# Letting ScalarE or VectorE copy Strassen banks out of PSUM, and three more stages of the last pairs turned on TensorE

## The chip, the core and the metric

The kernel runs on one core of a Trainium2 chip. The core has five engines, each with its own in-order queue: TensorE (PE, with its weight loads PEld), VectorE (DVE), ScalarE (ACT), GpSimd (POOL), and SyncE (SP), which here only issues DMAs. The metric is the device time of one execution in microseconds (us); lower is better.

## What is computed

There are 128 graphs of 128 nodes with 512 features. Four graph-attention layers follow each other, and each is added to its input and normalised over the features. In every layer the attention scores are a sum of two vectors, passed through a leaky ReLU, masked by the adjacency matrix and put through a softmax:

```python
x = _layernorm(x + L0(x, adj))   # attention on x itself, one head
x = _layernorm(x + L1(adj, x))   # two GAT layers inside: x@W1 (512->1024, 4 heads), elu, h@W2 (1024->512)
x = _layernorm(x + L2(x, adj))   # x@W (512->8 heads of 64), 8 heads of attention
x = _layernorm(x + L3(x, adj))   # scores from x@W_fc, attention on x, elu
# each attention:
e = leaky_relu(s_src[:, :, None] + s_dst[:, None, :], 0.2)
attn = softmax(where(mask, e, -inf)); out = attn @ h
```

All arithmetic is float32.

## The kernel before

The 128 graphs are handled as 64 pairs. A pair passes four stages, written as `first`, `second`, `third` and `fourth` in the kernel, with a dense projection between each two: by w1 after `first`, by w2 after `second`, by w3 after `third`. For a projection the two graphs of a pair are stacked, so that Strassen's scheme with seven products in place of eight can be used (`strassen`, Winograd's form). The w1 projection is two such schemes (two halves of the columns), w2 and w3 are one each, so a pair runs four schemes, 28 products.

Inside a scheme three PSUM banks are used, `pa`, `pb` and `pc`. I call the products p0 to p6 by the number of the weight slot that they read. p0 is written to `pa`, copied out (`taken`, first copy), and then `pa` is written again by p4, copied out, and added to by p5 and p6; `pb` gets p3, is copied out, and p2 is added; `pc` gets p1. That makes four copies of a scheme (three by `taken`, a last one straight to the result) and three additions (`added`, line 834). Every copy is made by `copied`, whose ScalarE instruction is line 797; the additions are VectorE's. The matmuls of the products are line 789. A product into `pa` or `pb` that follows a copy cannot start before that copy has read the bank. PSUM has 8 banks, and all matmul results of the kernel share them.

The attention of each head is: scores by ScalarE's PReLU into PSUM (line 719), mask and row minimum on VectorE (line 732, or 727 in the plain form), exponential with row sum on ScalarE (line 741), reciprocal (749). The layer's matmuls are lines 858, 949 and 1011, the normalisation is lines 760 to 780.

Two helpers move data across partitions. `spread` lays a column along every partition's row, `turned` transposes a block. Each has two forms. The usual one uses VectorE's 32x32 transposes (lines 638 and 692) and two DMAs by way of DRAM (642 and 648; 696 and 700 or 705). The quick one (`quick[0]` true) uses TensorE: lines 624 and 679, with copies out of PSUM at line 686. Which stages are quick is given by `QUICK`: its first number counts pairs at the start whose `first` is quick, the other four count pairs at the end whose `first`, `second`, `third` and `fourth` are.

The order of all work is computed when the program is built. Every step is an `Op` with an engine, a cost, and the buffers it reads and writes. `plan` gives each a due time from the longest path of costs behind it, stretched by `STRETCH` and shifted by `PACE` for each pair, `FIRST` for the first pairs and `SETUP` for the loading of the weights. `lay_out` then runs the engines forward in a model: of the ops that an engine could start, it takes the one that starts soonest, by due time where several could, not further ahead than `AHEAD`. The resulting order is fixed; on the chip each engine works through its own queue in that order and waits on semaphores. From about the twelfth pair on the order repeats itself exactly from pair to pair, with several pairs in flight at different stages; I call one such repetition a period.

Of the kernel before, what the change touches and what calls it, by code (L numbers as in the profile page):

```python
# [14 lines left out]
ALU = mybir.AluOpType  # L15
AX = mybir.AxisListType

P = 128
# [5 lines left out]

STRETCH, PACE, AHEAD = 1.28, 44.46, 61.8
HOP = {"PE": 0.0, "DVE": 0.0, "ACT": 0.5, "POOL": 1.0, "SP": 2.0}
SEED, SPREAD = 1, 0.0
SETUP = (-32.7, -34.3, 3.7)  # L30
QUICK = (2, 0, 0, 1, 2)
FIRST, LAST = (-64.8, -62.4, -109.6, -113.6, -123.5), ()
BANKS, PRODUCTS = 8, 2
SEES = {"PE": 0.06, "DVE": 0.06, "ACT": 0.06, "POOL": 0.06, "SP": 0.0}
TAIL = {"PE": 0.165, "DVE": 0.09, "ACT": 0.1, "POOL": 0.05, "SP": 0.0}
FLIGHT, LANDS, DESCRIBE = 1.3, 2.0, 0.00083
LANES = 8
SLACK = 2.0
REACH = 0.0
LOADS = (50.0, 12.8)  # L40


class Buf:
# [21 lines left out]
class Op:  # L65
# [3 lines left out]
    def __init__(self, engine, parts, emit, ins, outs, joins=(), uses=(), port=False, dma=0.0, due=0.0, gate=0.0, desc=0):  # L69
        self.desc = desc  # L70
        self.engine, self.emit = engine, emit
        self.parts = parts if isinstance(parts, list) else [parts]
        self.ins, self.outs, self.joins, self.uses = list(ins), list(outs), list(joins), list(uses)
        self.port, self.dma, self.due, self.gate = port, dma, due, gate
        self.lag, self.far = 0.0, 1.0 if any(b.tag.startswith("row") for b in self.ins) else 0.0
# [43 lines left out]
def lay_out(ops):  # L119

    n = len(ops)
    before = needs(ops)
# [11 lines left out]
    ready, ends, starts = [0.0] * n, [None] * n, [0.0] * n  # L134
    issued = [False] * n
    lane, landed, pool_until, vector_until, described = 0.0, [], 0.0, 0.0, 0.0

    def enter(i):
        op = ops[i]
        t = op.gate  # L140
        for q in before[i]:
            o = ops[q]
            if o.engine == op.engine != "SP":
                continue
            e = ends[q]
            t = max(t, (e[0] if len(e) == len(op.parts) > 1 else e[-1]) + SEES[o.engine] + (0.2 if op.engine == "PE" else 0.0))
        ready[i] = t
        insort(waiting[op.engine], (op.due, i))

    for i in range(n):  # L150
        if not missing[i]:
# [3 lines left out]
    while len(out) < n:  # L155
        for e, line in waiting.items():
            if e in choice or not line:
                continue
            free, best, limit = clock[e], None, ops[line_up[low]].due + AHEAD
            if e == "SP" and len(landed) >= LANES:  # L160
                free = max(free, landed[-LANES])
            for due, i in line:
                t = max(free, ready[i])
                if due > limit:
                    break
                if not ops[i].ins and due > limit - AHEAD + LOADS[due > 60.0]:
# [18 lines left out]
        waiting[e].remove((op.due, i))  # L185
        changed = False
        issued[i] = True
        while low < n and issued[line_up[low]]:
# [6 lines left out]
                    scarce[b.tag].pop(0)  # L195
                    changed = True
        now = max(now, t)
        starts[i] = u = t
        if e == "POOL":
            u = max(u, vector_until)  # L200
        got = []
# [27 lines left out]
        for q in after[i]:  # L229
            missing[q] -= 1  # L230
            if not missing[q]:
                enter(q)
                choice.pop(ops[q].engine, None)
        if changed:
            choice.clear()

# [25 lines left out]
def tile_gat_stack(  # L262
# [392 lines left out]
    def turned(srcs, n, moving=False, ordered=False):  # L655
# [5 lines left out]
        if quick[0]:  # L661
            for a, (b, src) in enumerate(srcs):
                if ordered:
                    own = Buf("own", [P, m, P])

                    def order(own=own, src=src, copy=(nc.vector.tensor_copy, nc.scalar.copy)[a % 2]):
                        copy(
                            own.ap.rearrange("p k (r b) -> p k r b", b=4),
                            src().rearrange("p k (b r) -> p k r b", b=4),
                        )  # L670

                    op(("DVE", "ACT")[a % 2], 0.06 + 0.137 * m, order, [b], [own])
                    b, src = own, lambda own=own: own.ap
                for lo in range(0, m, 4):
                    px, w = bank(), min(4, m - lo)

                    def flip(src=src, lo=lo, w=w, px=px):
                        for u in range(w):
                            nc.tensor.transpose(px.ap[:, u * P : (u + 1) * P], src()[:, lo + u, :], ident)

                    def taken(lo=a * m + lo, w=w, px=px, moving=moving, e=(lo // 4 + a) % 2):
                        to, got = o.ap[:, lo : lo + w, :], px.ap[:, : w * P].rearrange("p (h i) -> p h i", h=w)
                        if moving:
                            to = o.ap[:, :, lo : lo + w, :].rearrange("p q h c -> p h q c")
                            got = px.ap[:, : w * P].rearrange("p (h q c) -> p h q c", h=w, q=4)
                        (nc.vector.tensor_copy, nc.scalar.copy)[e](to, got)  # L686
# [24 lines left out]
    def attend(rows, src, mask, scaled=False):  # L711
# [38 lines left out]
        if scaled:  # L750
            op("POOL", 0.13 + 0.23 * nh, lambda: nc.gpsimd.tensor_mul(  # L751
                zz.ap, zz.ap, ri.ap.unsqueeze(2).to_broadcast([P, nh, P])
            ), [zz, ri], [zz])
        return zz, ri

    def norm(ys, plus=0.0):
# [22 lines left out]
        for g, (b, y) in enumerate(ys):  # L779
            op("ACT", 0.715, lambda g=g, y=y: nc.scalar.activation(  # L780
                y(), y(), AF.Identity, bias=mr.ap[:, g : g + 1], scale=rd.ap[:, g : g + 1]
            ), [b, rd, mr], joins=[b])
        return rd, md

    def chain(px, w, lhs, rhs, nk, ins, ready, fresh=True):
# [9 lines left out]

    def copied(px, w, to, joins=(), outs=()):
        op("ACT", 0.04 + w / 1200, lambda: nc.scalar.copy(to(), px.ap[:, :w]), [px], outs, joins)  # L797

    def project(lhs, wa, nk, w, n, to, t, ready):
        for c in range(n):  # L800
# [4 lines left out]
    def sums(left, shape):  # L805
# [4 lines left out]

        def summed(o, what, a, b):
            op("POOL", cost, lambda: nc.gpsimd.tensor_tensor(out=own[o][1](), in0=a[1](), in1=b[1](), op=what), [a[0], b[0]], [s[o]])  # L812

        (a11, a12), (a21, a22) = left
        summed(0, ALU.add, a21, a22)
# [5 lines left out]
    def strassen(left, s, w, nk, wide, cols, to, out, ready):  # L821
# [61 lines left out]
    def first(n):  # L883
# [37 lines left out]
        xT = turned([(b, lambda b=b: wide_rows(b.ap)) for b in x1], 8, ordered=True)  # L921
        for g in G:
            op("POOL", 1.24, lambda g=g: nc.gpsimd.tensor_add(x1[g].ap, x1[g].ap, b2t), [x1[g]], [x1[g]], uses=[b2b])
        return dict(xT=xT, xb=x1, m1=m1)

    def second(st, xl):
# [12 lines left out]
        for g in G:  # L939
            for c in range(2):  # L940
                op("POOL", 1.255, lambda g=g, c=c: nc.gpsimd.tensor_add(  # L941
                    xl[g].ap[:, c, : 2 * FH], xl[g].ap[:, c, : 2 * FH], b1t[:, c * 2 * FH : (c + 1) * 2 * FH]
                ), [xl[g]], [xl[g]], uses=[b1b])
            for c in range(2):
                pa, o = bank(), hT[g][c]

# [42 lines left out]
    def fourth(n, st, xl3):  # L989
# [10 lines left out]
        for g in G:  # L1000
# [4 lines left out]
            for q in range(2):  # L1005
# [16 lines left out]
            op("POOL", 1.17, lambda g=g: nc.gpsimd.tensor_add(  # L1022
                x3[g].ap.rearrange("p (h o) -> p h o", h=H2), z3[g].ap[:, :, :FO], x2[g].ap.rearrange("p (h o) -> p h o", h=H2)
            ), [z3[g], x2[g]], [x3[g]])
            op("DVE", 0.14, lambda g=g: nc.vector.tensor_reduce(
                out=sz.ap[:, g, :], in_=z3[g].ap[:, :, FO:].rearrange("p h s -> p s h"), op=ALU.add, axis=AX.X
            ), [z3[g]], joins=[sz])
# [21 lines left out]
            ), [y, pa], joins=[y])  # L1049
        for g in G:  # L1050
            op("POOL", 1.235, lambda g=g: nc.gpsimd.tensor_add(y.ap[:, g, :], y.ap[:, g, :], x3[g].ap), [y, x3[g]], joins=[y])  # L1051
        norm([part(y, g) for g in G])
        op("SP", 0.5, lambda: nc.sync.dma_start(
            out=out[2 * n : 2 * n + 2].rearrange("g p f -> p g f"), in_=y.ap
# [95 lines left out]
```

## Time and profile before

| | |
|---|---|
| runs shown | 3002.24, 3008.66, 3008.86 us, median 3008.66 |
| profiled execution: own time / span of instructions | 3002.53 / 3000.7 us |
| mean granted TensorE clock | 0.986 |
| busy: PE, PEld, DVE, ACT, POOL | 96%, 79%, 86%, 82%, 75% of the span |
| DMA | 594.74 MB, mean 198 GB/s |
| products w1, w2, w3 (line 789) | 803.3, 824.5, 472.6 us on PE |

A row of the groups gives line, engine, operation, what is written from what, its shape and count, then the total busy time, the mean time of one in ns, and the idle time of the engine ahead of them with what ended it. The mean time of one includes the tail of an instruction that overlaps the next; what an instruction really takes from a queue is the distance from its start to the next start, which the timeline gives. A row of the waits gives who waited for whom, the total, the number of times and the longest.

### The profile page before, as it was taken

Reading aid. Unit: us, or ns where it says so; the run is one execution under the profiler, and the core shown is the slowest. Engines: PE = TensorE matmul, PEld = TensorE weight load, DVE = VectorE, ACT = ScalarE, POOL = GpSimd, SP = SyncE. Lnnn points to the kernel's source line nnn. Section 1 sums busy time; section 2 is a strip of 40 time slices with the busy share of each in tenths; the row PEclk is TensorE's granted clock in tenths of the full one; section 3 lists DMA queues with packets and bytes.
Section 4 is the critical chain, followed back from the end, with each engine's and each line's share of the span. In section 5 each row is a group of like instructions: output and inputs, shape, how many; then the busy total and the mean of one; then the engine's idle time right before and its main releaser. Section 6 shows DMA issues by size and latency. Waiting matters only on the chain.

```text
span 3000.7 us, 56720 instructions
## 1 busy us (share of the span) xinstructions
PE 2884.1 (96%) x14200; PEld 2358.1 (79%) x14200; DVE 2592.1 (86%) x9256; ACT 2448.1 (82%) x8237; POOL 2244.7 (75%) x2855
## 2 busy tenths in 40 slices
PE   6999999999999999999999999999999999999986
PEld 4777778888888888888888888888888888888765
DVE  6788888898898899899889889889889988989875
ACT  3567888888888888888888888888888888888877
POOL 3886777877877787777777777777787777777654
PEclk8999999999999999999999999999999999999997
DMA  4469999999999998999989998999999899999863
GB/s 131 98 166 195 194 202 213 211 210 208 219 203 210 217 209 208 217 206 208 218 202 217 210 205 214 210 215 207 212 216 207 210 214 205 211 218 202 196 148 66
DMA packets 1465475, 594.74 MB, mean 198 GB/s; under 512 B 1251476, under 2 KB 1366932, under 8 KB 1465148
## 3 DMA queue, kind: packets, MB, share of 16 engines
q1 hardware_dynamic: 1464072, 589.54, 86.8%
q8 instruction: 115, 1.88, 0.3%
q14 instruction: 212, 1.74, 0.2%
q10 hardware_dynamic: 1076, 1.58, 0.2%
HBM read 367.88 MB, written 223.13 MB: 197 GB/s over the span
## 4 chain that ended last, share of the span: by engine, by line
PE 53%; ACT 21%; DVE 15%; DMA 5%; issue 4%; POOL 1%; SPq 0%; DVEq 0%; ACTq 0%; POOLq 0%
PE ps L789 37%; ACT ps L719 8%; PE ps L858 7%; PE ps L1011 6%; DVE arena L692 4%; ACT arena L741 3%; ACT arena L780 3%; DVE st L760 3%; ACT arena L956 3%; DVE arena L864 2%; ACT arena L797 2%; DVE arena L834 2%; DMA arena<-in_x_dram 2%; DVE arena L732 1%; DMA arena<-scr 1%
## 5 line engine op out<-in xcount | busy, mean ns | idle before, releaser
L789 PE MATMUL ps<-w2s,arena 128*128 128x257 f32 x3584 | 824.5, 381 | 13.4 <-DVE arena L957 9.8
L812 POOL TENSOR_TENSOR arena<-arena 128x256 f32<-128x256 f32 (+1 forms) x768 | 693.7, 915 | 189.8 <-DMA arena<-scr 114.6
L789 PE MATMUL ps<-w1s,arena 128*128 128x258 f32 x3584 | 803.3, 381 | 1.5 <-DVE arena L686 0.8
L789 PEld LDWEIGHTS ps<-w1s,arena 128*128 128x128 f32 x3584 | 680.1, 190 | 151.1 <-issue 39.9
L789 PEld LDWEIGHTS ps<-w2s,arena 128*128 128x128 f32 x3584 | 679.4, 190 | 148.1 <-issue 33.4
L741 ACT ACTIVATE arena<-arena,nm 128x128 f32<-128x128 f32 x1920 | 741.9, 395 | 14.8 <-DVE nm L732 8.7
L732 DVE CUSTOM_DVE_ANT_0 arena<-ps,arena 128x128 f32<-128x128 f32 x1878 | 520.9, 382 | 187.7 <-ACT ps L719 184.7
L719 ACT ACTIVATE ps<-arena 128x128 f32<-128x128 f32 x1504 | 552.6, 371 | 96.9 <-DMA arena<-row 59.8
L692 DVE STREAM_TRANSPOSE arena<-arena 128x512 f32<-128x512 f32 (+1 forms) x813 | 516.7, 637 | 47.3 <-POOL arena L751 31.2
L789 PE MATMUL ps<-w3s,arena 128*128 128x273 f32 x1792 | 472.6, 399 | 34.9 <-ACT arena L797 27.0
L797 ACT COPY arena<-ps 128x258 f32<-128x258 f32 (+2 forms) x1024 | 346.5, 376 | 190.4 <-PE ps L789 182.0
L780 ACT ACTIVATE arena<-arena,mr,rd 128x512 f32<-128x512 f32 x512 | 394.3, 806 | 31.4 <-POOL mr L776 31.4
L789 PEld LDWEIGHTS ps<-w3s,arena 128*128 128x128 f32 x1792 | 328.0, 191 | 107.5 <-issue 35.1
L858 PE MATMUL ps<-arena 128*128 128x512 f32 x768 | 374.3, 611 | 15.3 <-DVE arena L686 3.9
L741 ACT ACTIVATION_READ_ACCUMULATOR arena<-arena,nm 128x1 f32 x1920 | 372.9, 194 | 0.0
L869 POOL TENSOR_SCALAR arena<-arena 128x256 f32<-128x256 int32 x256 | 297.6, 1162 | 91.6 <-DMA arena<-in_adj_dram 51.1
L834 DVE TENSOR_TENSOR arena<-ps,arena 128x258 f32<-128x258 f32 (+2 forms) x768 | 312.9, 413 | 51.3 <-PE ps L789 45.0
L760 DVE BATCH_NORM_STATS2 st<-arena 128x6 f32<-128x512 f32 x512 | 341.5, 679 | 7.9 <-POOL arena L1022 2.1
L941 POOL TENSOR_TENSOR arena<-arena,b1t 128x512 f32<-128x512 f32 x256 | 320.9, 1283 | 0.3
L732 DVE DVE_READ_ACCUMULATOR2_ANT nm<- 128x1 f32 x1878 | 284.6, 152 | 0.0
L1051 POOL TENSOR_TENSOR arena<-arena 128x512 f32<-128x512 f32 x128 | 161.6, 1265 | 137.9 <-DVE arena L1047 130.3
L949 PEld LDWEIGHTS ps<-arena 128*128 128x128 f32 x2048 | 248.0, 192 | 15.2 <-issue 3.4
(96 smaller groups left out, 3622.2 us busy)
## 6 DMA issues: line engine op xcount, KB each, us to landing
scr<-arena SPq DMA_DIRECT2D x313, 512.0 KB
arena<-scr SPq DMA_DIRECT2D x313, 512.0 KB
arena<-row SPq DMA_DIRECT2D x188, 512.0 KB
arena<-in_x_dram SPq DMA_DIRECT2D x64, 512.0 KB
out_dram<-arena SPq DMA_DIRECT2D x64, 512.0 KB
arena<-row SPq DMA_DIRECT2D x187, 128.0 KB
scr<-arena SPq DMA_DIRECT2D x187, 128.0 KB
arena<-scr SPq DMA_DIRECT2D x187, 128.0 KB
```

Source lines behind the costliest of these rows:

```text
L692: op("DVE", 0.075 + 0.134 * m, lambda a=a, src=src: nc.vector.transpose(zb.ap[:, :, a * m : (a + 1) * m, :].rearrange("p b h c -> p h b c" ...
L719: nc.scalar.activation(z.ap[:, h * P : (h + 1) * P], rows[h][1](), AF.Prelu, bias=src[1]()[:, h : h + 1], alpha=SLOPE)
L732: nc.vector.tensor_tensor_reduce(out=zz.ap[:, h, :].rearrange("p (b a) -> p a b", b=4), in0=z.ap[:, h * P : (h + 1) * P].rearrange("p (a b ...
L741: nc.scalar.activation(zz.ap[:, h, :], zz.ap[:, h, :], AF.Exp, bias=nm.ap[:, h : h + 1], scale=-1.0, accum_out=rs.ap[:, h : h + 1],)
L760: op("DVE", 0.585, lambda g=g, y=y: nc.vector.bn_stats(st.ap[:, g, :], y()), [b], joins=[st])
L780: op("ACT", 0.715, lambda g=g, y=y: nc.scalar.activation(y(), y(), AF.Identity, bias=mr.ap[:, g : g + 1], scale=rd.ap[:, g : g + 1]), [b, ...
L789: nc.tensor.matmul(px.ap[:, :w], lhsT=lhs(k), rhs=rhs(k), start=(fresh and k == 0), stop=(k == nk - 1), skip_group_check=True,)
L797: op("ACT", 0.04 + w / 1200, lambda: nc.scalar.copy(to(), px.ap[:, :w]), [px], outs, joins)
L812: op("POOL", cost, lambda: nc.gpsimd.tensor_tensor(out=own[o][1](), in0=a[1](), in1=b[1](), op=what), [a[0], b[0]], [s[o]])
L834: op("DVE", 0.05 + wide / 960, lambda: nc.vector.tensor_add(to(g, h), px.ap[:, :wide], u.ap[:, :wide]), [px, u], joins=[out[g]])
L858: op("PE", 0.885, lambda: nc.tensor.matmul(pa.ap.rearrange("p (s c) -> p s c", s=2) if paired else pa.ap, lhsT=pt.ap[:, h, :], rhs=xv[1]() ...
L941: op("POOL", 1.255, lambda g=g, c=c: nc.gpsimd.tensor_add(xl[g].ap[:, c, : 2 * FH], xl[g].ap[:, c, : 2 * FH], b1t[:, c * 2 * FH : (c + 1) ...
```

## The change

A step may now name a second engine with its own cost (`or_on`), and `lay_out` puts it into both engines' lists; the engine that would end it sooner takes it, with a handicap of `EXTRA` = 0.2 us for the second one. Seven kinds of steps get such a second engine, always VectorE, but `FLEX` admits only one kind, "copy": the Strassen copies of `copied`. Two products of a scheme are written down in another order (p3 before p4, its copy before that of p4, p2 before p5). `QUICK` makes `second` of the last pair, `third` of the last two and `fourth` of the last three quick; before it was none, one and two. The constants of the planning change, and with them the order on every engine.

```diff
-STRETCH, PACE, AHEAD = 1.28, 44.46, 61.8
-HOP = {"PE": 0.0, "DVE": 0.0, "ACT": 0.5, "POOL": 1.0, "SP": 2.0}
+STRETCH, PACE, AHEAD = 1.26, 44.3, 58.4
+HOP = {"PE": 0.0, "DVE": 0.0, "ACT": 0.45, "POOL": 1.06, "SP": 2.0}
-SETUP = (-32.7, -34.3, 3.7)
-QUICK = (2, 0, 0, 1, 2)
-FIRST, LAST = (-64.8, -62.4, -109.6, -113.6, -123.5), ()
+SETUP = (-36.3, -10.6, -19.3)
+QUICK = (2, 0, 1, 2, 3)
+FIRST, LAST = (-64.8, -62.4, -117.1, -110.8, -116.1), ()
+EXTRA = 0.2
+FLEX = ("copy",)
-LOADS = (50.0, 12.8)
+LOADS = (46.3, 7.8)
...
+    def or_on(self, engine, cost, emit, port=False):
+        self.also = engine, cost if isinstance(cost, list) else [cost], emit, port
+
+    def switch(self):
+        mine = self.engine, self.parts, self.emit, self.port
+        self.engine, self.parts, self.emit, self.port = self.also
+        self.also = mine
...
+                if ops[i].also:
+                    op = ops[i]
+                    other = op.also[0] if e == op.engine else op.engine
+                    mine = sum(op.parts) if e == op.engine else sum(op.also[1])
+                    cost = sum(op.also[1]) if e == op.engine else sum(op.parts)
+                    if t + mine + (0.0 if e == op.engine else EXTRA) > max(clock[other], ready[other, i]) + cost + (EXTRA if e == op.engine else 0.0):
+                        continue
...
+    def either(name, engine, cost, emit, port=False):
+        if name in FLEX:
+            ops[-1].or_on(engine, cost, emit, port)
...
     def copied(px, w, to, joins=(), outs=()):
         op("ACT", 0.04 + w / 1200, lambda: nc.scalar.copy(to(), px.ap[:, :w]), [px], outs, joins)
+        either("copy", "DVE", 0.05 + w / 960, lambda: nc.vector.tensor_copy(to(), px.ap[:, :w]))
...
         taken(pa, t1)
         product(pc, left[0][1], 1, True)
         added(pc, t1, 0, 0)
+        product(pb, s[0], 3, True)
         product(pa, s[1], 4, False)
-        product(pb, s[0], 3, True)
+        taken(pb, v)
         taken(pa, u2)
-        taken(pb, v)
+        product(pb, s[3], 2, False)
         product(pa, s[2], 5, False)
-        product(pb, s[3], 2, False)
         added(pa, v, 1, 1)
```

More of the change, by code (lines that the diff above doesn't have):

```diff
@@ L74, in __init__ @@
         self.port, self.dma, self.due, self.gate = port, dma, due, gate
+        self.also = None
         self.lag, self.far = 0.0, 1.0 if any(b.tag.startswith("row") for b in self.ins) else 0.0
         self.bufs = list(dict.fromkeys([*self.ins, *self.outs, *self.joins, *self.uses]))
+    def or_on(self, engine, cost, emit, port=False):
[4 more added lines that the diff above has]
+        self.also = mine
     def least(self):
@@ L133, in lay_out @@
     waiting = {e: [] for e in TAIL}
-    ready, ends, starts = [0.0] * n, [None] * n, [0.0] * n
+    ready, ends, starts = {}, [None] * n, [0.0] * n
     issued = [False] * n
@@ L139, in enter @@
         op = ops[i]
[L140 to L148, printed above, removed]
+        for engine in [op.engine] + ([op.also[0]] if op.also else []):
+            t = op.gate
+            for q in before[i]:
+                o = ops[q]
+                if o.engine == engine != "SP":
+                    continue
+                e = ends[q]
+                t = max(t, (e[0] if len(e) == len(op.parts) > 1 else e[-1]) + SEES[o.engine] + (0.2 if engine == "PE" else 0.0))
+            ready[engine, i] = t
+            insort(waiting[engine], (op.due, i))
     for i in range(n):
@@ L162, in lay_out @@
             for due, i in line:
-                t = max(free, ready[i])
+                t = max(free, ready[e, i])
                 if due > limit:
                     break
+                if ops[i].also:
[4 more added lines that the diff above has]
+                    if t + mine + (0.0 if e == op.engine else EXTRA) > max(clock[other], ready[other, i]) + cost + (EXTRA if e == op.engine else 0.0):
+                        continue
                 if not ops[i].ins and due > limit - AHEAD + LOADS[due > 60.0]:
@@ L185, in lay_out @@
         waiting[e].remove((op.due, i))
+        if op.also:
+            other = op.also[0] if e == op.engine else op.engine
+            waiting[other].remove((op.due, i))
+            choice.pop(other, None)
+            if e != op.engine:
+                op.switch()
         changed = False
@@ L197, in lay_out @@
         now = max(now, t)
-        starts[i] = u = t
+        op.start = starts[i] = u = t
         if e == "POOL":
@@ L233, in lay_out @@
                 choice.pop(ops[q].engine, None)
+                if ops[q].also:
+                    choice.pop(ops[q].also[0], None)
         if changed:
@@ L681, in taken @@
                     def taken(lo=a * m + lo, w=w, px=px, moving=moving, e=(lo // 4 + a) % 2):
-                        to, got = o.ap[:, lo : lo + w, :], px.ap[:, : w * P].rearrange("p (h i) -> p h i", h=w)
                         if moving:
@@ L685, in taken @@
                             got = px.ap[:, : w * P].rearrange("p (h q c) -> p h q c", h=w, q=4)
+                        else:
+                            to, got = o.ap[:, lo : lo + w, :], px.ap[:, : w * P].rearrange("p (h i) -> p h i", h=w)
                         (nc.vector.tensor_copy, nc.scalar.copy)[e](to, got)
@@ L753, in attend @@
             ), [zz, ri], [zz])
+            either("zz", "DVE", 0.08 + 0.138 * nh, lambda: nc.vector.tensor_mul(
+                zz.ap, zz.ap, ri.ap.unsqueeze(2).to_broadcast([P, nh, P])
+            ), True)
         return zz, ri
@@ L782, in norm @@
             ), [b, rd, mr], joins=[b])
+            either("norm", "DVE", 0.62, lambda g=g, y=y: nc.vector.tensor_scalar(
+                out=y(), in0=y(), scalar1=rd.ap[:, g : g + 1], scalar2=mr.ap[:, g : g + 1], op0=ALU.mult, op1=ALU.add
+            ), True)
         return rd, md
@@ L812, in summed @@
             op("POOL", cost, lambda: nc.gpsimd.tensor_tensor(out=own[o][1](), in0=a[1](), in1=b[1](), op=what), [a[0], b[0]], [s[o]])
+            either("sum", "DVE", 0.08 + s[0].size / 930, lambda: nc.vector.tensor_tensor(out=own[o][1](), in0=a[1](), in1=b[1](), op=what), True)
         (a11, a12), (a21, a22) = left
@@ L923, in first @@
             op("POOL", 1.24, lambda g=g: nc.gpsimd.tensor_add(x1[g].ap, x1[g].ap, b2t), [x1[g]], [x1[g]], uses=[b2b])
+            either("b2", "DVE", 0.62, lambda g=g: nc.vector.tensor_add(x1[g].ap, x1[g].ap, b2t), True)
         return dict(xT=xT, xb=x1, m1=m1)
@@ L943, in second @@
                 ), [xl[g]], [xl[g]], uses=[b1b])
+                either("b1", "DVE", 0.62, lambda g=g, c=c: nc.vector.tensor_add(
+                    xl[g].ap[:, c, : 2 * FH], xl[g].ap[:, c, : 2 * FH], b1t[:, c * 2 * FH : (c + 1) * 2 * FH]
+                ), True)
             for c in range(2):
@@ L1024, in fourth @@
             ), [z3[g], x2[g]], [x3[g]])
+            either("x3", "DVE", 0.62, lambda g=g: nc.vector.tensor_add(
+                x3[g].ap.rearrange("p (h o) -> p h o", h=H2), z3[g].ap[:, :, :FO], x2[g].ap.rearrange("p (h o) -> p h o", h=H2)
+            ), True)
             op("DVE", 0.14, lambda g=g: nc.vector.tensor_reduce(
@@ L1051, in fourth @@
             op("POOL", 1.235, lambda g=g: nc.gpsimd.tensor_add(y.ap[:, g, :], y.ap[:, g, :], x3[g].ap), [y, x3[g]], joins=[y])
+            either("y", "DVE", 0.62, lambda g=g: nc.vector.tensor_add(y.ap[:, g, :], y.ap[:, g, :], x3[g].ap), True)
         norm([part(y, g) for g in G])
```

## The prediction

> **What bounds the kernel now.** I read the page's busy shares first, then the stretches, then the waits of each engine, then the timeline around the longest-repeated wait. The stretches, with the busy time of PE, PEld, DVE, ACT and POOL in us, the granted clock and the DMA share:
>
> ```profile
> 1500.00:2000.00 500.00, 492.23 (x2457) 405.33 (x2456) 448.51 (x1602) 426.55 (x1453) 386.93 (x494) 1.00 0.92 210
> ...
> 2850.00:2900.00 50.00, 44.17 (x206) 35.72 (x206) 32.14 (x120) 35.28 (x116) 30.58 (x41) 0.91 0.81 177
> 2900.00:2925.00 25.00, 20.71 (x89) 14.64 (x87) 21.10 (x81) 20.63 (x72) 10.77 (x21) 0.86 0.34 90
> ...
> 2975.00:3001.00 26.00, 9.36 (x20) 4.22 (x20) 10.77 (x30) 14.58 (x30) 9.60 (x19) 0.70 0.27 91
> ```
>
> In the middle PE is busy 98.4% of the time at full clock, VectorE 89.7%, ScalarE 85.3%. Between the first w3 matmuls of pairs 14 and 54 the trace has 40 periods in 1779.7 us, 44.49 us each; PE is idle in 0.69 us of one (7.77 of 500). So the most that the repeating part can give is about 0.69 x 52 = 36 us, plus what the two ends hold. What ends PE's idle time, over the whole run:
>
> ```profile
> PE ps L789 <- ACT arena L797: 27.0, 52, 2.4
> PE ps L679 <- ACT arena L667: 17.2, 3, 11.3
> PE ps L789 <- DMA arena<-scr: 5.7, 1, 5.7
> ```
>
> The first row is one place met once a period, 0.52 us each: p4 of the w3 scheme waits until ScalarE has copied p0 out of the same bank. The other two are single stalls, at the start and at 2873 us. ScalarE's queue up to that copy:
>
> ```profile
> 1490.49 0.69 ACT L1045 ACTIVATE arena<-ps,minus 128x512 f32<-128x512 f32 x1 [2.52 <-PE ps L858]
> ...
> 1505.87 0.77 ACT L719 ACTIVATE ps<-arena,sc 128x128 f32<-128x128 f32 x2
> 1506.57 0.64 ACT L797 COPY arena<-ps 128x258 f32<-128x258 f32 x2
> 1507.10 0.30 ACT L769 ACTIVATE rd<-mv,eps 128x2 f32<-128x2 f32 x1
> ...
> 1512.11 0.68 ACT L797 COPY arena<-ps 128x273 f32<-128x273 f32 x2
> ```
>
> ScalarE is ahead of PE at 1490.49 (it had waited 2.52 us for L858) and behind it 21.6 us later, with no idle time between that shows. PE's side:
>
> ```profile
> 1511.78 0.38 PE L909 MATMUL ps<-ident,arena 128*128 128x128 f32 x2
> 1512.65 0.47 PE L789 MATMUL ps<-w3s,arena 128*128 128x273 f32 x1 [0.48 <-ACT arena L797]
> ```
>
> PE was done at 1512.16 and started p4 at 1512.65. So in each period PE hands over to ScalarE's queue here, and that queue is 0.48 us too long.
>
> **Step 1: the copies that change engine.** The order of the built program shows 447 of the 1024 copies on VectorE: 415 of 512 for w1, 9 of 256 for w2, 23 for w3. In the repeating part it is seven of a period's eight w1 copies and none other. Starts one after another give what each costs its queue: two ScalarE copies from 1506.57 to 1507.10, 0.265 us each. A VectorE copy of this size is not in the trace; the nearest row is the addition that also reads a bank, which takes
>
> ```profile
> 1501.10 0.74 DVE L834 TENSOR_TENSOR arena<-ps,arena 128x258 f32<-128x258 f32 x2
> 1501.76 0.74 DVE L864 SCALAR_TENSOR_TENSOR arena<-ps,ri,arena 128x512 f32<-128x512 f32 x1
> ```
>
> 0.66 / 2 = 0.33 us. The cheapest VectorE row that reads as much from PSUM (L912, 128x256) is followed by the next start after 0.31, the mean duration of L834 is 0.41; I take 0.33, with 0.31 and 0.41 as ends. ScalarE: 7 x 0.265 = 1.86 us less in a period, from 37.8 to 36.0. VectorE: 7 x 0.33 = 2.3 us more (2.2 to 2.9), from 39.9 to 42.2 of 44.49, 95%.
>
> *A rule against this.* The Trainium skill, page Perfetto Trace Analysis, section Optimizing Scalar/DVE Operations, says that an operation pays a fixed cost of about 125 ns on VectorE and about 51 ns on ScalarE when it touches PSUM, and that work should go from VectorE to ScalarE when VectorE is saturated. This change goes the other way, onto the busier engine. By its figures a copy would be an estimated 51 + 258/1.2 = 266 ns on ScalarE, as the row says, and 125 + 258/0.96 = 394 ns on VectorE, where the row of an addition says 330; VectorE would then stand at an estimated 42.7 us of a period.
>
> **Step 2: the wait at p4.** I sum ScalarE's queue from the first y-exponential (L1045) to the copy of p0 of w3, in both orders. Costs by distance of starts: L1045 and L956 0.57, L719 0.385, L741 0.385 with its accumulator read, L780 0.705, L769 with L770 0.42, a copy 0.265. Before: 2 L1045, 18 L719, 18 L741, 8 copies, 3 pairs L769/770, 2 L780, 3 L956 = 1.14 + 6.93 + 6.93 + 2.12 + 1.26 + 1.41 + 1.71 = 21.5, and the trace had 21.6. After: 2 L1045, 16 L719, 20 L741, 1 copy, 2 pairs, 2 L780, 3 L956 = 1.14 + 6.16 + 7.70 + 0.27 + 0.84 + 1.41 + 1.71 = 19.2. PE's queue over the same stretch holds the same matmuls in both orders, 21.7 us in the trace. So the copy would be ready 1.8 us before PE comes, instead of 0.5 after. Against it: the exponentials L741 wait for masks (L732), which now stand on VectorE behind the moved copies. At worst all seven delay them, 2.3 us, and the wait stays at 0.5; at best it is gone. Most of the seven lie between masks that ScalarE's PReLUs (L719) have not fed yet, where VectorE idles now, so I take the wait as gone in full, 27 us, and give back 5 us (0.1 a period) for small waits that the tighter VectorE queue makes. Steady part: -22 us, with ends 0 and -36. The reordered products change no matmul; p2 of w3 now stands last instead of fifth, so `pb` is held longer by two products, 0.93 us at 0.232 a matmul; with eight banks I cost it at nothing; if a bank is short, that is up to 0.93 us in a period, and it counts with the slower rival.
>
> **Step 3: the start.** The 11.3 us stall (at 62 to 73 us) ends with pair 1's normalisation; in the new order GpSimd still runs two scalings (L751) ahead of it, so it stays. The preparation of w2 on GpSimd stands later: from that normalisation to its last subtraction (L374) 38 us of GpSimd work instead of 25; but PE now has 52 us of matmuls ahead of the first product that needs it instead of 36, since pair 2's w1 was moved up. Covered: 0. Without that cover it would be 13 us; with luck the filling stage, where PE idles 16.5 us between 150 and 500 against 5.4 for the same length later, gives up to 6. Ends -6 and +6.
>
> **Step 4: the end.** Three more stages become quick: 28 more spreads by matmul (8.3 us / 34 = 0.24 each) and 36 more transposes (16.5 us / 66 = 0.25): 6.8 + 9.0 = 15.8 us more on PE. Off it go 21 DMAs on SP's queue, which has little else in the tail, and ten transposes L692 on VectorE. PE is idle 33 us after 2850, so the added work may all lie in gaps: the 5.7 us stall at 2873 is ahead of pair 61's w3, which the new order puts behind pair 63's w2. But after the last w1 copy ScalarE has 126 us of work against 119 before by the costs above, and PE 125 against 108, in a stretch that took 159: the chain to the end is shorter for the last pair and fuller for the engines. I take 0, with -12 (the stalls of 5.7 and 4.0, and 2 us in which cold matmuls followed the first) and +16 (all added PE work in series).
>
> The first w3 matmuls behind the 5.7 us stall took 3.98 us for eight, where eight elsewhere take 1.9. The Trainium skill, TensorE: Matmul & The Clock Gate, Part 1, says the clock halves after some 3.4 us of idle time; by it each such gap costs an estimated 1.7 us or more beyond itself, so a stall that returns in the fuller tail would be dearer than its length.
>
> **Sum.** 3002.5 (profiled execution) - 22 + 0 + 0 = 2980.5. The median of the runs is 6 us above that execution, the lowest run equal to it; I put the forecast half way, +3.5: 2984.
>
> **The rivals.** *VectorE becomes the bound* (slower). It idles 4.7 us in a period now, of which 3.0 are masks waiting for PReLUs (L732 <- L719, 133.5 us in 45 periods). If those waits stay in series, VectorE needs 42.2 + 3.0 = 45.2 us, +0.7 in a period, +36 us in 52: 3002.5 + 36 + 3.5 = 3042. With all its idle time it would be 46.9 and +125. It decides as soon as more than 2.3 us of VectorE's waits stay. Against it: a mask waits because VectorE comes early, and with seven copies ahead it comes later.
> *The wait only moves* (same): p4 waits for masks instead of copies, or the tail takes back what the middle gives: -9 to +9 us, about 3006.
> *More than the visible wait* (much faster): all of PE's 0.69 us goes, and -12 in the tail, -6 at the start: 3002.5 - 54 + 3.5 = 2952.
>
> **How the numbers follow.** Forecast case (-9 to -35 us) 0.45; much faster 0.11; within 0.3% (9 us, about what a measurement here tells from no change) 0.14; slower 0.30. Faster in all 0.56. The slower case's mass lies mostly in its first 30 us, since the lower half of its waits must survive for more. The range 2952 to 3034 leaves out some 0.06 below and 0.12 above; the forecast case alone would be 2968 to 2997.
>
> **What would show it.** Right: a period near 44.05 us; in PE's waits the row with L797 for w3 gone or below 8 us; ScalarE near 78% and VectorE near 92% of the span busy; copies on VectorE 0.31 to 0.41 apart. Wrong: a new row in which PE waits for VectorE (L834 or the new copy) over 20 us; a period above 44.5; a VectorE copy dearer than 0.41; PE idle over 45 us after 2850.

## The result and the profile after

The changed kernel takes 2963.64 us (median of 4 runs, 2963.17 to 2966.57), the kernel before 3007.83 (4 runs, 3002.24 to 3008.86): ratio 0.9859, interval 0.9842 to 0.9876. The profiled execution of the changed kernel took 2964.05 us, with a span of 2962.3. It is faster, as forecast, by 44 us where 24 were forecast.

Lines have moved: the products 789 are now 829, the ScalarE copy 797 is 837, the VectorE copy is 838, the addition 834 is 876, PReLU 719 is 753, mask 732 is 766, the sums 812 on GpSimd are 853, the score dots 898 are 940.

The busy shares of the page after:

```profile
PE 2892.2 (98%) x14292; PEld 2360.1 (80%) x14292; DVE 2762.8 (93%) x9694; ACT 2326.7 (79%) x7795; POOL 2213.1 (75%) x2855
```

VectorE rose from 86% to 93% and ScalarE fell from 82% to 79%, near the 92% and 78% that the prediction named. The stretches, with the columns of the prediction's:

```profile
1500.00:2000.00 500.00, 495.18 (x2467) 405.79 (x2466) 483.11 (x1692) 403.04 (x1360) 388.38 (x495) 1.00 0.94 211
...
2850.00:2900.00 50.00, 49.94 (x276) 41.46 (x275) 36.66 (x152) 41.87 (x143) 23.78 (x37) 1.00 0.44 85
2900.00:2925.00 25.00, 22.68 (x142) 19.91 (x142) 17.66 (x93) 24.00 (x97) 8.16 (x13) 0.82 0.02 7
2925.00:2963.00 38.00, 17.54 (x79) 10.84 (x77) 21.28 (x70) 28.23 (x70) 19.98 (x43) 0.81 0.21 76
```

In the middle PE is idle 4.8 of 500 us instead of 7.8, and VectorE, at 483 of 500, is nearly as full as PE. In the tail PE is busy without a gap and at full clock up to 2900, where before it ran at 0.91 with 6 us idle. What ends PE's idle time, over the whole run:

```profile
PE ps L829 <- DVE arena L876: 19.7, 46, 3.2
...
PE ps L829 <- ACT arena L837: 1.3, 3, 0.9
```

The wait for ScalarE's copy has gone from 27.0 us to 1.3. In its place stands a row in which PE waits for VectorE's addition. 16.3 us of it are met at one product of w3, about once a period (44 times); 3.2 are a single stall at a w1 product while the pipeline fills.

**Where the time went.** I split each span at three points: the first w3 matmul of pair 14, that of pair 54 (40 periods later), and the end of the last w1 matmul. All values are us, from the profiled execution.

| | to pair 14 | a period | pair 54 to last w1 | last w1 to end | span |
|---|---|---|---|---|---|
| before | 796.3 | 44.49 | 265.0 | 159.8 | 3000.7 |
| changed | 784.9 | 44.25 | 260.9 | 146.5 | 2962.3 |
| e1 all copies on ScalarE | 796.1 | 45.00 | 266.5 | 149.1 | 3011.5 |
| e2 before, seven copies on VectorE | 814.4 | 46.15 | 275.1 | 158.1 | 3093.7 |
| e3 old QUICK | 786.6 | 44.32 | 262.9 | 159.8 | 2982.1 |
| e4 old start | 787.3 | 44.36 | 261.4 | 147.7 | 2971.0 |
| e5 changed again | 786.5 | 44.24 | 260.4 | 148.3 | 2964.7 |
| e6 addition before dot | 782.6 | 43.94 | 258.4 | 148.2 | 2946.7 |
| e7 no choice of engine | 798.6 | 45.48 | 277.8 | 147.7 | 3043.2 |
| e8 dot planned at 1.1 us | 786.0 | 44.21 | 263.8 | 147.0 | 2965.0 |
| e9 before, new QUICK | 801.4 | 44.64 | 266.3 | 159.8 | 3012.9 |
| e10 e6, more quick | 783.5 | 44.16 | 285.0 | 146.4 | 2981.2 |

From before to changed: -11.4 in the start, -9.7 in 40 periods, -4.1 in the last pairs and -13.3 after the last w1. Kernels whose order is the same in the middle (changed, e3, e4, e5; before and e9; e6 and e10) differ there by up to 0.22 us a period, so a difference of 0.2 in that column between two runs is no evidence by itself. The 0.24 from before to changed is hardly more; it rests on the two groups, 44.49 and 44.64 for the order of before, 44.24 to 44.36 for that of the changed kernel. In the start, before and e9 differ by 5.1 us and the kernels with the changed start (changed, e3, e5) by 1.7. Part of this is the chip: the kernel before took 3015.22 us on that of e1 to e4, 3010.49 on that of e5 to e8 and 3013.91 on that of e9 and e10. Ratios below are to the kernel before on the same chip.

### The profile page after: what moved, and what is told of

It reads as the page before. It is cut to its first block, busy times and chain, and to the rows that moved or that the text cites. A ratio compares the mean times of both kernels' runs of the same rounds, so it can differ in the third digit from the quotient of the medians.

```text
span 2962.3 us, 56920 instructions
## 1 busy us (share of the span) xinstructions
PE 2892.2 (98%) x14292; PEld 2360.1 (80%) x14292; DVE 2762.8 (93%) x9694; ACT 2326.7 (79%) x7795; POOL 2213.1 (75%) x2855
## 5 line engine op out<-in xcount | busy, mean ns | idle before, releaser
L829 PE MATMUL ps<-w2s,arena 128*128 128x257 f32 x3584 | 834.5, 384 | 3.6 <-DVE arena L1003 2.1
L829 PEld LDWEIGHTS ps<-w2s,arena 128*128 128x128 f32 x3584 | 667.8, 190 | 119.1 <-POOL arena L853 18.2
L753 ACT ACTIVATE ps<-arena 128x128 f32<-128x128 f32 x1480 | 538.7, 370 | 53.9 <-DMA arena<-row 15.0
L726 DVE STREAM_TRANSPOSE arena<-arena 128x512 f32<-128x512 f32 (+1 forms) x803 | 497.3, 630 | 24.8 <-ACT arena L775 4.6
L766 DVE CUSTOM_DVE_ANT_0 arena<-ps,arena 128x128 f32<-128x128 f32 x1850 | 501.8, 379 | 13.9 <-ACT ps L753 10.2
L829 PE MATMUL ps<-w3s,arena 128*128 128x273 f32 x1792 | 471.7, 398 | 20.7 <-DVE arena L876 16.5
L837 ACT COPY arena<-ps 128x257 f32<-128x257 f32 (+2 forms) x577 | 205.4, 375 | 245.4 <-PE ps L829 245.1
L900 PE MATMUL ps<-arena 128*128 128x512 f32 x768 | 376.7, 602 | 3.2 <-DVE arena L720 2.9
L775 ACT ACTIVATION_READ_ACCUMULATOR arena<-arena,nm 128x1 f32 x1920 | 361.8, 188 | 0.0
L984 POOL TENSOR_TENSOR arena<-arena,b1t 128x512 f32<-128x512 f32 x256 | 349.8, 1371 | 10.8 <-DVE b1t L500 3.3
L876 DVE TENSOR_TENSOR arena<-ps,arena 128x258 f32<-128x258 f32 (+2 forms) x768 | 306.0, 412 | 35.3 <-PE ps L829 18.4
L812 POOL TENSOR_TENSOR md<-mv,rd 128x2 f32<-128x2 f32 x256 | 54.0, 211 | 374.3 <-ACT rd L807 357.3
```

The costliest lines, as they stand in the source:

```text
L726: op("DVE", 0.075 + 0.134 * m, lambda a=a, src=src: nc.vector.transpose(zb.ap[:, :, a * m : (a + 1) * m, :].rearrange("p b h c -> p h b c" ...
L753: nc.scalar.activation(z.ap[:, h * P : (h + 1) * P], rows[h][1](), AF.Prelu, bias=src[1]()[:, h : h + 1], alpha=SLOPE)
L766: nc.vector.tensor_tensor_reduce(out=zz.ap[:, h, :].rearrange("p (b a) -> p a b", b=4), in0=z.ap[:, h * P : (h + 1) * P].rearrange("p (a b ...
L775: nc.scalar.activation(zz.ap[:, h, :], zz.ap[:, h, :], AF.Exp, bias=nm.ap[:, h : h + 1], scale=-1.0, accum_out=rs.ap[:, h : h + 1],)
L829: nc.tensor.matmul(px.ap[:, :w], lhsT=lhs(k), rhs=rhs(k), start=(fresh and k == 0), stop=(k == nk - 1), skip_group_check=True,)
L876: op("DVE", 0.05 + wide / 960, lambda: nc.vector.tensor_add(to(g, h), px.ap[:, :wide], u.ap[:, :wide]), [px, u], joins=[out[g]])
```

## Experiment group 1: is it the engine, or the order?

**e1** keeps the order of the changed kernel on every engine but lets ScalarE make the 447 copies after all:

```diff
             if e != op.engine:
                 op.switch()
+                op.emit = op.also[2]
```

> The order and the placing of all work are those of the changed kernel; only the 447 copies given to VectorE are made by ScalarE after all, at the same place of the order. Theory A (ScalarE's queue ahead of p4 was the cost, and relieving it is the gain): ScalarE's queue from the y-exponential to the copy of p0 grows from 19.2 to about 21.1 us against PE's 21.7, so waits of PE for line 837 copies come back and the period rises from 44.25 to 44.4 or more; time 2970 to 2990. Rival B (VectorE, 97% busy in the middle, is now the bound): the period falls under 44.0 and the time under 2955. Rival C (the new places in the order matter, the engine does not): within 9 us of 2964.

Measured: 3013.1 us, ratio 0.9994 (0.9985 to 1.0003); period 45.00, start 796.1. PE's waits between 500 and 2500 us, in e1:

```profile
PE ps L830 <- DVE arena L877: 14.1, 39, 0.5
PE ps L830 <- ACT arena L838: 10.1, 21, 0.9
```

So without the other engine the new order is worth nothing in all, and the time lies beyond the 2990 that Theory A allowed: the gain of the middle goes away with 0.75 us a period against the changed kernel, and that of the start with 11.2 us; only that after the last w1 stays (149.1). But the place is not the one that the prediction had named. At p4 of w3 PE loses little in e1 as well (0.10 us a period, by the distances of starts that the last section explains): the new order itself removed that wait. What ScalarE is late for in e1 are the w1 copies: about 0.7 us of PE's lost time in a period lies at w1 products, where the changed kernel loses 0.03.

**e2** is the reverse: the order of before, with seven of each pair's eight w1 copies made by VectorE.

```diff
+    turn = [0]
...
+        turn[0] += w == C1
+        copy = nc.vector.tensor_copy if w == C1 and turn[0] % 8 else nc.scalar.copy
-        op("ACT", 0.04 + w / 1200, lambda: nc.scalar.copy(to(), px.ap[:, :w]), [px], outs, joins)
+        op("ACT", 0.04 + w / 1200, lambda: copy(to(), px.ap[:, :w]), [px], outs, joins)
```

> The order of the kernel before, with seven of every eight w1 copies made by VectorE at the same place of the order. Theory A: ScalarE's queue ahead of p4 is shortened by up to 1.9 us, the 27 us of waits of PE for line 797 go, and the time falls from 3003 to between 2970 and 2985. Rival B: VectorE's queue, unplanned for the copies, stalls PE, and the time is over 3010. Rival C: the engine does not matter, within 9 us of 3005.

Measured: 3095.54 us, ratio 1.0264 (1.0248 to 1.0279), 1.66 us a period dearer; of the three expectations Rival B holds. PE's waits between 500 and 2500 us, in e2:

```profile
PE ps L789 <- ACT arena L801: 34.6, 30, 1.2
PE ps L789 <- POOL arena L873: 14.3, 12, 1.2
PE ps L789 <- DVE arena L801: 6.5, 12, 1.5
```

The first row is ScalarE's copies, now longer waits than the 20.3 us that the same window of before shows, although ScalarE has fewer of them. Behind it stands ScalarE's own wait for the masks, its exponentials L741 for L732. In the same window, before and e2:

```profile
ACT arena L741 <- DVE nm L732: 4.6, 16, 0.7
...
ACT arena L741 <- DVE nm L732: 119.9, 44, 2.9
```

That is the fear of step 2 ("masks, which now stand on VectorE behind the moved copies"), come true where nobody placed the copies. The copies must be planned for VectorE, not only moved to it.

**e7** plans anew with the constants of the change, but with no choice of engine:

```diff
-FLEX = ("copy",)
+FLEX = ()
```

> The changed kernel with FLEX empty: all copies on ScalarE, the order planned for that, all new constants and quick stages kept. Theory A (the choice of engine is the gain of the middle): period 44.4 to 44.8, 8 to 30 us over e5. Rival R (the new constants alone gave it): within 6 us of e5.

Measured: 3045.69 us, ratio 1.0118 (1.0103 to 1.0133); period 45.48. That is 80 us over e5, far beyond the 8 to 30 of Theory A. The new constants, with the new order of the products, are not what makes the middle faster: without the choice they are worse than those of before. No run gives the kernel before the choice alone, so how much the constants and the order of the products add to the choice is open.

## Experiment group 2: the new wait

The prediction named as a sign of being wrong "a new row in which PE waits for VectorE (L834 or the new copy) over 20 us"; there is one of 19.7, just below. Its main place, in the timeline of the changed kernel, VectorE:

```profile
1539.33 0.68 DVE L940 CUSTOM_DVE_ANT_0 arena<-arena,w0d 128x512 f32<-128x512 f32 x1
...
1539.94 1.75 DVE L940 CUSTOM_DVE_ANT_0 arena<-arena,w0d 128x512 f32<-128x512 f32 x1
...
1545.91 1.67 DVE L940 CUSTOM_DVE_ANT_0 arena<-arena,w0s,b0t 128x512 f32<-128x512 f32 x1
...
1547.51 0.43 DVE L876 TENSOR_TENSOR arena<-ps,arena 128x273 f32<-128x273 f32 x1
1547.87 1.40 DVE L940 CUSTOM_DVE_ANT_0 arena<-arena,w0s,b0t 128x512 f32<-128x512 f32 x1
```

PE in the same stretch:

```profile
1545.70 1.90 PE L829 MATMUL ps<-w2s,arena 128*128 128x257 f32 x8
1547.99 1.19 PE L829 MATMUL ps<-w3s,arena 128*128 128x273 f32 x4 [0.39 <-DVE arena L876]
```

The second PE row is p6 of the w3 scheme. It waits for the addition L876, which had waited in VectorE's queue behind a dot of 1.67 us. GpSimd in the same stretch tells why the dot is so long:

```profile
1539.49 1.65 POOL L853 TENSOR_TENSOR arena<-arena 128x512 f32<-128x512 f32 x1 [0.65 <-DVE arena L1003]
...
1543.28 3.75 POOL L853 TENSOR_TENSOR arena<-arena 128x512 f32<-128x512 f32 x3
1546.99 1.72 POOL L984 TENSOR_TENSOR arena<-arena,b1t 128x512 f32<-128x512 f32 x1
```

The three GpSimd spells end at 1541.14, 1547.03 and 1548.71; the three long dots end at 1541.69, 1547.58 and 1549.27. Each ends 0.55 or 0.56 us after the GpSimd operation beside it, however early it began; the dot at 1539.33, which began before that operation, took 0.68. The whole trace has 256 dots: 189 begin while a GpSimd operation runs, and four in five of them end 0.546 to 0.552 us after it; the other 67 take 0.69 us in the median.

**e6** leaves the change as it is, but on VectorE this addition (marked `soon`) goes ahead of the dot that stood before it (marked `dot`), in 54 pairs:

```diff
+        for k in range(len(order)):
+            if getattr(order[k], "soon", False):
+                j = max(q for q in range(k) if order[q].engine == "DVE")
+                late = order[j]
+                if getattr(late, "dot", False) and not any(set(late.outs + late.joins) & set(o.bufs) for o in order[j + 1 : k]):
+                    del order[j]
+                    order.insert(k, late)
...
```

> The changed kernel with one swap on VectorE in each of 54 pairs: the addition that frees the w3 bank for p6 goes ahead of the score dot product (the w0s one) that stands before it, all else in place. Theory P (p6 waits, 0.6 us in a period with its hidden part, because that addition stands behind a dot product which GpSimd holds up to 1.3 to 1.7 us): the row of PE waiting for line 876 falls from 14 us in the middle to under 4, the period from 44.25 to between 43.6 and 43.9, the time by 15 to 30 us against e5. Rival Q (VectorE, 97% busy, is the bound by its amount of work, so a swap on it gives nothing): within 6 us of e5, with another wait on VectorE in place of that one.

Measured: 2953.0 us, ratio 0.9811 (0.9793 to 0.9828), against 0.9855 (0.984 to 0.9869) for **e5**, the changed kernel again on the same chip.

> The changed kernel itself, on the chip and in the rounds of the three that follow, as their base. All theories: 0.984 to 0.988 of the kernel before.

e5 measured 2965.95 us. PE's waits between 500 and 2500 us, in e6:

```profile
PE ps L829 <- DVE arena L838: 3.0, 10, 0.5
PE ps L829 <- ACT arena L837: 2.5, 11, 0.4
```

The row of the addition (14.0 us in this window of the changed kernel) is gone, and 5.5 us of other waits came instead. At 13 us less than e5, e6 is faster than both kernels: the new wait had taken back about that much. VectorE is no less busy for it, 487 of 500 us in the middle, so it was the place of the one addition and not the amount of work on VectorE (Rival Q). How large the gain is in a period is less sure: 43.94 here, but 44.16 in e10, which has the same order in the middle.

**e8** tells the planner that a dot costs 1.1 us, near what the trace of before has (1.01 and 1.12 in the mean), in place of 0.63. It does not make the model truer: `lay_out` already lets a dot (`port=True`) wait until the GpSimd operation laid out before it is over (`u = max(u, pool_until)`) and then adds the cost, so that 1.1 counts part of that wait twice.

```diff
-                op("DVE", 0.63, lambda g=g, s=s, wv=wv, init=init, jk=jk: nc.vector.tensor_tensor_reduce(
+                op("DVE", 1.1, lambda g=g, s=s, wv=wv, init=init, jk=jk: nc.vector.tensor_tensor_reduce(
```

> The changed kernel with the planned cost of a score dot product raised from 0.63 to 1.1 us, near the 1.27 us that they take in the trace beside GpSimd; the whole order is planned anew. Theory P: a plan that knows of the long dot products keeps urgent work clear of them, period 43.7 to 44.1, 5 to 25 us under e5. Rival Q: the load is the same, within 8 us of e5 or slower by the luck of the new order.

Measured: 2969.89 us, ratio 0.9868 (0.9851 to 0.9884), no gain over e5. The new plan did keep half of the dots clear of GpSimd:

```profile
L940 DVE CUSTOM_DVE_ANT_0 arena<-arena,w0s,b0t 128x512 f32<-128x512 f32 x90 | 109.1, 1212 | 0.0
...
L940 DVE CUSTOM_DVE_ANT_0 arena<-arena,w0d 128x512 f32<-128x512 f32 x90 | 59.0, 692 | 0.0
```

VectorE came down to 463 of 500 us in the middle, and yet one row of PE's waits (500 to 2500 us) is as large as the old one:

```profile
PE ps L829 <- ACT arena L837: 16.9, 44, 0.9
```

The plan avoided the wait for VectorE and made one for ScalarE's copies in w3, at p4 and p2. Less work on VectorE does not by itself make a better order; moving the one late instruction (e6) did.

## Experiment group 3: the two ends

**e3** is the changed kernel with the old `QUICK`; its order on TensorE is that of the changed kernel up to matmul instruction 6752 of 7263.

```diff
-QUICK = (2, 0, 1, 2, 3)
+QUICK = (2, 0, 0, 1, 2)
```

> The changed kernel with QUICK as it was (the order is the same up to PE's matmul 6752 of 7263, only the last pairs differ). Theory E (the three quick stages shorten the end): the 17 us that the trace shows from pair 54's w3 to the end come back, time 2976 to 2984. Rival (the end gained from the copies and the new due times, as the prediction's step 4 costed the quick stages at nothing): within 5 us of 2964.

Measured: 2982.39 us, ratio 0.9888 (0.9872 to 0.9904). The profiled span is 19.8 us longer than the changed kernel's, 13.3 of them after the last w1, where it is at 159.8 again, exactly before's. The timed ratios differ by less, 0.9888 against 0.9855 or 0.9859, which is 9 to 10 us. So the three quick stages do shorten the end of the changed kernel (Theory E), by 10 to 20 us.

**e4** undoes the planning of the start (`SETUP` and `FIRST`; the new `LOADS` stay):

```diff
-SETUP = (-36.3, -10.6, -19.3)
+SETUP = (-32.7, -34.3, 3.7)
-FIRST, LAST = (-64.8, -62.4, -117.1, -110.8, -116.1), ()
+FIRST, LAST = (-64.8, -62.4, -109.6, -113.6, -123.5), ()
```

> The changed kernel with SETUP and FIRST as they were (LOADS stays new, for memory; PE's order is the same from about matmul 1500 of 7263 on). Theory S (the new due times of weights and first pairs gave the 11 us by which pair 14's w3 comes earlier): time 2971 to 2979. Rival (they gave nothing; the fill is faster because of the copies): within 4 us of 2964.

Measured: 2973.37 us, ratio 0.9858 (0.9844 to 0.9872), the changed kernel's own; the time itself lies in the range of Theory S only because the chip was slower. Its start takes 787.3 us against 784.9: some 2.4 of the start's 11.4 us may be these constants, little more than the 1.7 by which runs of one start differ. With e1 (796.1) the rest is the choice of engine, at work in the first pairs already.

**e9** asks whether the new `QUICK` pays in the kernel before. It needs `SLACK` 1.8 for its buffers to fit, and one branch of the quick `turned` as the changed kernel has it (not shown); its order on TensorE is before's up to instruction 6886 of 7199.

```diff
-QUICK = (2, 0, 0, 1, 2)
+QUICK = (2, 0, 1, 2, 3)
...
-SLACK = 2.0
+SLACK = 1.8
...
```

> The kernel before, every copy on ScalarE, with the new QUICK alone (second of the last pair, third of the last two and fourth of the last three quick) and, so that its buffers fit, SLACK 1.8 for 2.0; the order on TensorE is before's up to matmul instruction 6886 of 7199. Theory: the quick stages are worth 15 us by themselves, as taking them out of the changed kernel cost 15 us (422.7 against 407.4 us from the first w3 matmul of pair 54 to the end); then this stretch goes from 424.8 to about 410 us and the ratio to the kernel before is about 0.995. Rival: the quick stages pay only because the copies on VectorE have relieved ScalarE in the tail; then the stretch stays within 5 us of 424.8 and the ratio within 0.9983 and 1.0017.

Measured: 3014.44 us, ratio 0.9995 (0.9986 to 1.0004); 426.1 us from pair 54's w3 on, 159.8 after the last w1. The theory fell, and the rival's numbers hold, but not its reason: e7 has no copy on VectorE at all and e1 none either, and both end in 147.7 and 149.1 us after the last w1. So the quick stages need something else of the change (`STRETCH`, `PACE`, `AHEAD`, `HOP`, `SETUP`, `FIRST`, `LOADS` or the order of the products; `SLACK` is a further difference), not the second engine. The stretch from the last w1 to the end, in before, in six parts added up (PE, PEld, DVE, ACT, POOL busy, in us; 160 us in all):

```profile
sum 160.00, PE 124.14 PEld 96.66 DVE 98.94 ACT 119.61 POOL 75.38; mean PE 20.69 PEld 16.11 DVE 16.49 ACT 19.93 POOL 12.56
```

The same of e9, with its last two parts:

```profile
2953.00:2978.00 25.00, 20.42 (x81) 15.85 (x79) 14.32 (x60) 21.48 (x83) 6.49 (x15) 0.57 0.02 7
2978.00:3013.00 35.00, 16.32 (x50) 9.52 (x49) 17.68 (x57) 22.67 (x55) 17.40 (x32) 0.70 0.23 82
sum 160.00, PE 133.47 PEld 106.94 DVE 95.34 ACT 121.86 POOL 72.60; mean PE 22.25 PEld 17.82 DVE 15.89 ACT 20.31 POOL 12.10
```

And of the changed kernel, 147 us:

```profile
2916.00:2941.00 25.00, 20.44 (x104) 16.92 (x104) 14.96 (x54) 22.78 (x81) 12.35 (x29) 0.73 0.07 27
2941.00:2963.00 22.00, 6.09 (x14) 2.31 (x14) 11.69 (x31) 14.45 (x30) 11.35 (x17) 0.78 0.29 102
sum 147.00, PE 124.15 PEld 102.15 DVE 98.05 ACT 116.12 POOL 73.63; mean PE 20.69 PEld 17.03 DVE 16.34 ACT 19.35 POOL 12.27
```

I divide PE's busy time into work and what the clock took, by an estimate: in each part, busy time times one minus the granted clock. Before: 17.7 us to the clock, 106.4 of work, 35.9 idle. e9: 15.2, 118.2, 26.5. Changed: 6.9, 117.3, 22.9. So both kernels with the new `QUICK` have 11 to 12 us more work on PE. In e9 the filled gaps and a little clock pay for exactly that: 0. In the changed kernel the filled gaps give 13.0 and the clock 10.8: 11 - 24 = -13. The clock is granted in full until 2916 there, and 26.5 us of PE time are left when it falls to 0.73 and 0.78; in e9 the last 60 us hold 37 us of PE time at 0.57 and 0.70. Which of the differences does it was not taken apart.

**e10** gives e6 one more quick pair in `second`, `third` and `fourth`:

```diff
-QUICK = (2, 0, 1, 2, 3)
+QUICK = (2, 0, 2, 3, 4)
```

> The kernel e6 (changed kernel, on VectorE the addition that frees the bank for p6 of w3 ahead of the dot) with QUICK (2, 0, 2, 3, 4): second, third and fourth quick for one more pair each. Theory: the gain of quick stages came from filling TensorE's gaps in the last 150 us; TensorE is idle there for only 23 us now, so one more pair each puts about 16 us of TensorE work where few gaps are left: the end from pair 54's w3 goes from 406.6 to 406 to 412 us, ratio to the kernel before 0.981 to 0.983. Rival: the gain is the shorter chain of DMAs of each quick stage, which goes on with every pair: another 8 us or more off the end, below 399 us, ratio about 0.9785.

Measured: 2982.99 us, ratio 0.9895 (0.9875 to 0.9916), 431.4 us from pair 54's w3: dearer than either theory had it. After the last w1 it takes 146.4 us, no less than e6; the loss is ahead of it, 285.0 against 258.4, because in this order the w1 of the last pair starts 64.9 us after that of the pair before (e6: 43.3). Some 10 us more lie in the part where its order is e6's, so the loss against e6 is partly the spread of these runs.

## Why the prediction was right and wrong

The sign held, and so did its first reason, that ScalarE's queue is relieved by the second engine (e1, e7). The place where this pays was not the one priced, and the sum was 20.4 us short. 16.5 of these are terms (-38.5 against -22), 3.9 the offset to the median (+3.5 assumed, -0.4 found).

*Step 1 held.* 317 copies of 258 columns on VectorE in the 45 periods from 500 to 2500 are seven a period:

```profile
L838 DVE COPY arena<-ps 128x258 f32<-128x258 f32 x317 | 123.2, 414 | 14.6 <-PE ps L829 13.9
```

Where nothing holds VectorE, the next instruction starts 0.33 us after such a copy (mean of 236); 0.33 was taken. Of the 414 ns of the mean duration a part overlaps the next instruction. The Trainium skill's page Perfetto Trace Analysis, section Optimizing Scalar/DVE Operations, gave an estimated 394 ns for it; as the price of a place in the queue that was too much, and the measurement decides. Of the move to ScalarE the page says only that it "may make sense" when VectorE is saturated; here the reverse paid.

*Step 2: the mechanism was half right, the size too large.* "I take the wait as gone in full, 27 us, and give back 5 us (0.1 a period)". The wait at p4 did go (27.0 to 1.3), but e1 shows that the new order removed it even with every copy on ScalarE, and by the prediction's own sum it had to: 19.2 + 1.86 = 21.1 us of ScalarE's queue against PE's 21.7. And 16.3 us came back at p6, not 5. The period is 44.25, not the forecast 44.05. That is the rival "the wait only moves", which was to move it to masks; it moved to a dot. By the distances of starts, before loses 0.71 us a period at p4 and 0.52 at the attention products L858; the changed kernel loses 0.09 at p4, nothing at those products (now L900), 0.62 at p6 and 0.39 ahead of w2 products. So p6 took back what p4 gave, 0.62 each, and the 0.24 that is left comes from the other places, L858 above all, for which the prediction had no term. What the copies themselves are worth shows in e1, at the w1 products. The term that was missing: the dots of VectorE. By form, from 500 to 2500 us, before:

```profile
L898 DVE CUSTOM_DVE_ANT_0 arena<-arena,w0s,b0t 128x512 f32<-128x512 f32 x90 | 101.0, 1123 | 0.0
L898 DVE CUSTOM_DVE_ANT_0 arena<-arena,w0d 128x512 f32<-128x512 f32 x90 | 90.5, 1006 | 0.5 <-DMA arena<-in_x_dram 0.5
```

and after:

```profile
L940 DVE CUSTOM_DVE_ANT_0 arena<-arena,w0s,b0t 128x512 f32<-128x512 f32 x90 | 133.0, 1478 | 0.0
L940 DVE CUSTOM_DVE_ANT_0 arena<-arena,w0d 128x512 f32<-128x512 f32 x90 | 104.4, 1197 | 0.0
```

(32.0 + 13.9) / 45 = 1.0 us a period more on VectorE for the same instructions, because in the new order they meet longer work of GpSimd (before: 227 dots begin beside a GpSimd operation and take 1.01 us in the median; after: 189, which take 1.57). VectorE's busy time in the middle rose to 42.8 us of a period instead of the forecast 42.2. The row was in the trace of before, at 1.0 to 1.1 us where a dot takes 0.68 without a wait, and the prediction gave it no term.

*VectorE as the bound* did not come, since its waits for PReLUs did not stay. From 500 to 2500 us, before, changed and e2:

```profile
DVE arena L732 <- ACT ps L719: 133.5, 215, 1.4
...
DVE arena L766 <- ACT ps L753: 0.8, 3, 0.3
...
DVE arena L732 <- ACT ps L719: 150.2, 212, 2.6
```

The copies fill the time in which masks were not yet fed, as step 2 argued. e2 shows what happens when they lie elsewhere: those waits stay, and it is 2.6% slower. That rival was a fact of the placing, not of the load.

*The bank of p2.* "`pb` is held longer by two products, 0.93 us at 0.232 a matmul" was reckoned wrong: a product of w3 is four rows of the trace, so two are eight, 1.86 us. It was costed at nothing, so the sum does not change.

*Step 3: mis-sized, 0 against -11.4* (below its end of -6). It priced two stalls and the preparation of w2, and counted the gain of step 2 only for 52 periods. The stall of 11.3 us went in the changed kernel, and e4 has one of 9.5 in that place and is only 2.4 us later at pair 14, so that such a stall costs little here; e1 puts the rest with the copies, which help while the pipeline fills as well.

*Step 4: mis-sized, 0 against -13.3 after the last w1* (-12 was its end). "The chain to the end is shorter for the last pair and fuller for the engines" was right: 11 us more work on PE, where 15.8 was reckoned. What had no term in the sum is the clock: PE without gaps kept it, which gave back about as much as was added (by the estimate of group 3). The prediction used the rule of the Trainium skill, TensorE: Matmul & The Clock Gate, Part 1, only as a danger (a stall that returns is dear); by the same rule a gap that is filled can be worth more than its length, and the rows go that way: 13 us less idle, 11 us less lost to the clock. But e9 shows the sign was not to be had from this alone: the same quick stages with another order gave 0.

Taken together the steady part and the start gave -25.2 (-11.4 - 9.7 - 4.1) where -22 was forecast for both, a sum that came out nearly right from a term too large (0.42 a period taken, 0.24 found) and one left out.

## What to carry to other kernels

A copy can go to the busier engine and still pay, if it is placed where that engine waits: what counts is what stands behind it in the queue, and much the same copies gave -1.4% in an order made for them (changed against e1) and +2.6% in one that was not (e2 against before). After such a move look for the next late instruction in the filled queue; moving a single addition ahead of a long dot was worth another 13 us in e6, though e10 leaves the size open. A change that fills the gaps of TensorE near the end must be priced with the clock that it keeps, and tried with the order it will run in.

## What was not expected of the hardware

In the rows of group 2 the same dot took 0.68 us, or 1.4 to 1.75 where a GpSimd operation ran when it began, and then it ended 0.55 us after that operation did. The Trainium skill, SBUF — State Buffer, section SBUF: two separate sides, says that a VectorE operation with two SBUF inputs and a GpSimd operation that reads SBUF take a shared pair of ports as an exclusive lock, so that the later one blocks for the other's whole instruction. The rows above and the 189 dots agree with it; a proportional slowing would not end each dot at the same distance from the other's end. That is also what the kernel's `port=True` models.

PE's idle time shows too little of a wait. A product's matmul row lasts 0.38 us while such matmuls start 0.22 us apart when nothing holds them, so the first 0.16 us of a wait lie under the row before it and count as busy. The sum of these median distances over a period's matmuls (for the two transposes by `ident` the 0.11 us that they take when nothing holds them) is 43.2 to 43.3 us in each of seven kernels (before, changed, e1, e2, e6, e7, e8); before was 1.26 us above it, with only 0.68 us of idle time shown, the changed kernel 1.02 with 0.37, and e6 0.71. "The most that the repeating part can give is about 0.69" was therefore too low a bound.
